# Softmax sums of two attention layers: from matmuls with ones to sums of exponentials along the query's row

## The chip, the cores and the metric

The kernel runs on one core of a Trainium2 chip. The metric is the device time in microseconds of one execution, as the median of several runs. A core has a matrix engine (TensorE, PE in the profile; PEld is its weight load), VectorE (DVE), ScalarE (ACT), GpSimd (POOL) and SyncE (SP), whose queue issues the DMAs here. Matrix results go to PSUM, of which there are eight banks of 128 partitions by 512 fp32 words; all else lives in SBUF.

## The reference

Four cross-attention layers follow each other on `x` (8 batches, 256 tokens, 512 features), with a context of the same shape. What matters here are the first layer and the fourth, which are ordinary attention with 16 heads of 32 features:

```python
# layer 0: layer norm, attention over the context, output projection, residual, then a feed-forward with gelu
scores = jnp.einsum('bhqd,bhkd->bhqk', q, k) * scale
scores = jnp.where(mask, scores, mask_value)
attn = jax.nn.softmax(scores, axis=-1)
out = jnp.einsum('bhqk,bhkd->bhqd', attn, v)
...
# layer 3: the context is layer-normed; Q from the hidden state, K and V from the context
scores = jnp.einsum('bhtd,bhsd->bhts', Q, K) * scale
scores = jnp.where(mask, scores, jnp.float32(-jnp.inf))
attn = jax.nn.softmax(scores, axis=-1)
out = jnp.einsum('bhts,bhsd->bhtd', attn, V)
return hidden_states + jnp.tanh(gate) * (out @ Wo.T)
```

The second layer is a single-head attention, the third has 32 query heads of 16 features on 8 key heads with an added mask.

## The kernel before

**Numbers in two parts.** Most products are done on pairs: a value is split into a rounded part and the rest (`hi`, `lo`), and three passes of matmuls join them (`feat_mm`, `tok_mm`).

**Units.** The attention of the first and fourth layer is cut into 32 units each, one for a batch and four heads (class `Mha`). `load` brings queries and keys of a unit into two tiles of the ring `stack` (in the fourth layer also `st` and `ks`), whose rows 0 to 95 hold the parts of the 32 features and whose further rows hold the mask and the maxima.

- `A(h)`, for each of the four heads: two matmuls give the scores of 256 queries (on partitions, in two halves) by 256 keys in an `sm` bank, of which there are two; VectorE takes the negative maximum of each query (`negm`, 128x2). After the last head GpSimd splits the eight columns of maxima into two parts (`mhl`).
- `B`: TensorE transposes `mhl`, ScalarE copies the result to `mT`, and a DMA writes it into rows 97 and 98 of the queries' tile, where the keys' tile holds ones.
- `C(i)`, four steps: matmuls give the scores again, now with keys on partitions and the maximum subtracted by the extra rows, in an `st` bank; ScalarE takes the exponential into the tile `P`. `P` of two heads and one half of the keys is one step.
- `AV(kt)`, one for each half of the keys: for each head the matmul of `P` with 32 columns of values into the bank `av`, columns 0 to 255, and a matmul of `P` with 32 columns of ones into columns 256 to 511: the sums of the softmax, repeated over the 32 partitions of the head. Each of these matmuls uses 32 columns of the array; four heads have four places side by side.
- `D`: the reciprocal of the sums (by Ln and Exp on ScalarE, or on VectorE while ScalarE's table for tanh is loaded), the product, and the split of the result into `at`, from which the projection of the batch is made.

The values stand in memory with their ones, 96 columns for two heads (`values`, `v0d`, `v3d`); the tile `V` holds 768 columns for each half of the keys.

**Order.** `pipeline` goes through the units: in step t it emits `A` of unit t, `B` of unit t-1 and `C` and `D` of unit t-2. `A` and `C` have a high priority; between them `fill.tick` emits filler work by a budget in microseconds (`B0` in the first layer, `B3` in the fourth): projections of later batches, the folded weights, the first feed-forward steps. The whole program is then put in order by a list scheduler with a model of the engines, so that the emitted order is a wish only. `Burst` asks it to issue the matmuls of a run one behind the other (`tc.issue_after` and a high priority). Each engine executes its own queue in order; an instruction that waits holds everything behind it on that engine.

**Slots.** SBUF is cut into named slots (a, b, c, v of fixed sizes); each phase has a table (`A0_SB`, `L_SB`, `L3_SB`) that says which slots a kind of tile goes through in turn. A tile's DMA or first write waits until the last reader of the slot's previous tile is done.

## Time and profile before

| | |
|---|---|
| median of 3 runs | 1755.96 us (1746.53, 1758.2, 1755.96) |
| profiled execution | 1749.14 us |
| its span, first to last instruction | 1747.4 us |
| mean granted clock of TensorE | 0.958 |
| TensorE / VectorE / ScalarE / GpSimd busy | 92% / 62% / 49% / 42% |
| value matmuls of the two layers (L588, 128x256) | 136.9 us busy, 2048 records |
| reductions to the maxima (L640) | 169.8 us, 256 |
| exponentials into `P` (L677) | 145.7 us, 256 |
| reciprocals on VectorE (L698) | 36.8 us, 21 |

How to read it: a busy time is the time in which at least one instruction of the group ran. Durations can overlap, on TensorE above all, so a mean duration times a count can be more than the busy time. "Idle before" is the time an engine stood still ahead of the group, with the instruction that released it. A row that begins with a time comes from the timeline: start and length in microseconds, engine, line, operation, tiles. Line numbers are those of the kernel before unless the text says that they belong to the changed one.

### The profile page before, as it was taken

The numbers are of one execution on the slowest core, as the hardware profiler recorded it, in microseconds if no ns is written. First come the engines' busy times: TensorE is split into PE (matmuls) and PEld (weight loads), VectorE is DVE, ScalarE is ACT, GpSimd is POOL, SyncE is SP. The second block draws the span as 40 slices with busy tenths as digits, with TensorE's granted clock in tenths as the row PEclk, the third lists the DMA queues.
The fourth block names the chain that finished last, engine by engine and source line by source line (L and its number), as shares of the span: only waits on it lengthen the run. The fifth ranks groups of instructions, "written<-read, shape, count | busy, mean of one in ns | idle before, by whom it ended". The sixth has DMA issues, their size and how long they took to land.

```text
span 1747.4 us, 28230 instructions
## 1 busy us (share of the span) xinstructions
PE 1616.0 (92%) x9984; PEld 1224.4 (70%) x9984; DVE 1085.8 (62%) x2412; ACT 864.0 (49%) x1531; POOL 731.1 (42%) x760
## 2 busy tenths in 40 slices
PE   7999999999799999999689899898878989999998
PEld 6877867777577878878456576666646767777765
DVE  6258557777757766622567577666777785655433
ACT  5336545554446566632255456454455545544444
POOL 6345145333455565531234445444436563422111
PEclk9999999999999999999789899898989999999999
DMA  8979775555632434285654575656366756776662
GB/s 294 319 240 285 220 234 190 164 153 164 188 129 88 146 119 145 77 290 218 196 175 151 190 240 174 202 177 189 97 198 180 231 164 217 213 220 210 192 182 76
DMA packets 168444, 329.16 MB, mean 188 GB/s; under 512 B 16336, under 2 KB 84336, under 8 KB 162800
## 3 DMA queue, kind: packets, MB, share of 16 engines
q1 hardware_dynamic: 168304, 327.35, 59.1%
q8 instruction: 80, 1.31, 0.3%
q14 instruction: 60, 0.49, 0.1%
HBM read 230.79 MB, written 96.49 MB: 187 GB/s over the span
## 4 chain that ended last, share of the span: by engine, by line
PE 64%; DMA 15%; DVE 9%; ACT 4%; issue 3%; POOL 3%; SPq 2%; DVEq 0%; ACTq 0%; POOLq 0%
PE pp L212 21%; PE pp L226 21%; PE av L588 8%; PE st L669 3%; PE sm L633 3%; PE st L1233 3%; PE sm L1179 2%; DMA stack<-mT 2%; DMA nat<-in_ctxT_dram 2%; DVE sm L1189 1%; DMA ws<-mnd 1%; PE pp L336 1%; PE pp L1143 1%; DMA stack<-q0d 1%; DMA nd<-avd 1%
## 5 line engine op out<-in xcount | busy, mean ns | idle before, releaser
L640 DVE TENSOR_REDUCE negm<-sm 128x2 f32<-128x512 f32 x256 | 169.8, 682 | 125.4 <-PE sm L633 124.7
L677 ACT ACTIVATE P<-st 128x512 f32<-128x512 f32 x256 | 145.7, 594 | 126.5 <-PE st L669 125.0
L212 PE MATMUL pp<-ys,fw 128*128 128x512 f32 x768 | 190.9, 398 | 6.3 <-ACT fw L178 3.8
L226 PE MATMUL pp<-pw,gs 128*128 128x512 f32 x768 | 193.3, 398 | 3.1 <-ACT gs L948 2.6
L212 PE MATMUL pp<-x,wq 128*128 128x256 f32 x1152 | 169.4, 291 | 6.9 <-ACT wq L181 3.1
L212 PEld LDWEIGHTS pp<-ys,fw 128*128 128x128 f32 x768 | 144.0, 191 | 40.4 <-ACT fw L178 4.0
L212 PEld LDWEIGHTS pp<-x,wq 128*128 128x128 f32 x1152 | 156.2, 196 | 20.5 <-issue 6.6
L226 PEld LDWEIGHTS pp<-pw,gs 128*128 128x128 f32 x768 | 142.1, 190 | 38.5 <-ACT gs L948 4.2
L588 PE MATMUL av<-P,V 128*32 128x256 f32 (+1 forms) x2188 | 164.5, 402 | 4.0 <-DVE xt L702 2.9
L1189 DVE CUSTOM_DVE_ANT_0 sm<-sm,va 128x256 f32<-128x256 f32 x256 | 104.8, 440 | 56.2 <-PE sm L1179 55.1
L1179 PE MATMUL sm<-ks,stack 96*128 96x512 f32 x256 | 111.4, 467 | 29.2 <-DMA stack<-q2d 16.3
L949 POOL TENSOR_TENSOR gs<-xt,gs 128x512 fp32r<-128x512 f32 x64 | 91.8, 1442 | 90.8 <-ACT gs L948 90.8
L1189 DVE CUSTOM_DVE_ANT_0 sm<-sm,vb 128x256 f32<-128x256 f32 x256 | 104.4, 440 | 37.8 <-PE sm L1179 36.5
L1233 PE MATMUL st<-stack,ks 100*128 100x512 f32 x256 | 103.7, 459 | 18.2 <-DMA stack<-mT 10.0
L1248 ACT ACTIVATE P<-P 128x1024 f32<-128x1024 f32 x90 | 95.1, 1059 | 50.3 <-POOL P L1244 26.0
L226 PE MATMUL pp<-wo,at 128*128 128x512 f32 x384 | 106.5, 404 | 1.3 <-ACT at L705 1.3
L944 DVE SCALAR_TENSOR_TENSOR xt<-xt,xt 128x512 f32<-128x512 f32 x64 | 66.6, 1045 | 64.5 <-ACT xt L943 64.5
L588 PEld LDWEIGHTS av<-P,V 128*32 128x32 f32 x2188 | 59.0, 109 | 57.6 <-issue 15.4
L179 POOL TENSOR_TENSOR fw<-stg,fw 128x1024 fp32r<-128x1024 f32 x32 | 81.8, 2564 | 34.7 <-ACT fw L178 19.6
L1179 PEld LDWEIGHTS sm<-ks,stack 96*128 96x128 f32 x256 | 51.5, 207 | 63.4 <-issue 30.0
L645 POOL CAST mhl<-negm 128x8 fp32r<-128x8 f32 x64 | 15.9, 249 | 187.7 <-DVE negm L640 187.7
L226 PEld LDWEIGHTS pp<-wo,at 128*128 128x128 f32 x384 | 69.8, 191 | 22.7 <-issue 3.3
(214 smaller groups left out, 3557.0 us busy)
## 6 DMA issues: line engine op xcount, KB each, us to landing
stg<-in_wfc_dram SPq DMA_DIRECT2D x32, 512.0 KB
stg<-in_wpr_dram SPq DMA_DIRECT2D x32, 512.0 KB
ws<-med SPq DMA_DIRECT2D x16, 1024.0 KB
ws<-mnd SPq DMA_DIRECT2D x16, 1024.0 KB
q2d<-nat SPq DMA_DIRECT2D x48, 256.0 KB
stack<-q2d SPq DMA_DIRECT2D x32, 384.0 KB
k0d<-nat SPq DMA_DIRECT2D x16, 512.0 KB
stack<-k0d SPq DMA_DIRECT2D x32, 256.0 KB
```

What stands on the lines that cost most here:

```text
L179: lo.tensor_tensor(w[:, 1], stg, fp(w[:, 0]), ALU.subtract)
L212: nc.tensor.matmul(pt[:, :n], lhsT=sel(ws, wj, kc)[:, ft * P : (ft + 1) * P], rhs=sel(xs, xj, kc), start=(k == 0), stop=(k == 11),)
L226: nc.tensor.matmul(pt[:, :n], lhsT=sel(xs, xj, kc)[:, tt * P : (tt + 1) * P], rhs=sel(ws, wj, kc), start=(k == 0), stop=(k == 11),)
L588: self.prev = nc.tensor.matmul(o, lhsT=lhsT, rhs=rhs, start=start, stop=stop, skip_group_check=True).ins
L640: nc.vector.tensor_reduce(self.negm[:, 2 * h : 2 * h + 2], pt.rearrange("p (q k) -> p q k", q=2), AX.X, ALU.max, negate=True)
L677: nc.scalar.activation(p, pt, AF.Exp)
L944: nc.vector.scalar_tensor_tensor(v, v, 1.0 / GA, u, ALU.add, ALU.mult)
L949: nc.gpsimd.tensor_tensor(lo, u, fp(hi), ALU.subtract)
L1179: nc.tensor.matmul(pts[qt], lhsT=self.qs[0:96, h, qt * P : (qt + 1) * P], rhs=self.ks[0:96].rearrange("p u k -> p (u k)"), start=True, sto ...
L1189: nc.vector.tensor_tensor_reduce(out=t, in0=t, in1=self.am[:, qt, :], scale=1.0, scalar=-3.0e38, op0=ALU.add, op1=ALU.max, accum_out=self. ...
L1233: nc.tensor.matmul(pt, lhsT=self.ks[0:100, u, kt * P : (kt + 1) * P], rhs=self.qs[0:100, 2 * hp : 2 * hp + 2, :].rearrange("p h t -> p (h ...
L1248: last["act"] = nc.scalar.activation(pf, pf, AF.Exp).ins
```

## The change

The sum of the exponentials is formed in `A`, where the scores stand with the queries on partitions: behind the reduction, ScalarE takes the exponential of each half of the bank with the negative maximum as its bias, back into the same bank, and writes the sum of the row (`sums`, 128x8 for a unit). `shift` takes the logarithm of the eight columns and subtracts it from the negative maximum; this difference is split into `mhl` and goes the way of the maximum's row. With it the exponentials in `C` give probabilities that add up to one, so the matmuls with ones, the reciprocal and the product are left out. While the table for tanh is loaded, the logarithm comes from an estimate by the bits of the number and a polynomial: nine VectorE operations on 128x8 and one exponential.

With it: `AV` goes into `D` as one run of eight matmuls, heads 0 to 3 for the first half of the keys, then for the second; the copy to `mT` and the first part of the result move from ScalarE to VectorE, the second part in the fourth layer from GpSimd to VectorE; the values lose their ones (512 columns instead of 768), in the fourth layer they come in two tiles in slots c0, c1, c3, c4, and `P` has five slots there instead of three; the mask's number is zero for a batch that is wholly masked.

```diff
@@ -55,7 +55,10 @@
     return o
 
 
-SMALL = dict(sm1=8, st6=4, negm=3, mhl3=3, mhl=2, mx=2, mT=3)
+SMALL = dict(sm1=8, st6=4, negm=3, sums=3, lg=6, mhl3=3, mhl=2, mx=2, mT=3)
+
+LN2 = 0.6931471805599453
+LGA, LGB = LN2 / 2.0**23, -LN2 * (127.0 - 0.0430357)
 C0_SB = dict(wk="a0-1", wv="a6-7", wq="a8-9", xs="a2-5", x8="a10-11", stg="b0-2", nat="b3-6", vo="b7-8,v0",
              h="b9-10", xt="c0-3", bc="c4-5", m="c6-8")
 A0_SB = dict(stack="a12-15", wc="a0-1", w8="a2-5", x8="a10-11", at="a6-7", stg="b3,b4,b6",
@@ -66,8 +69,8 @@
 L_SB = dict(wq="a12-13", wo="a0-1", ws="a8-9,a2", x8="a4-5,a3", ec="a6", pk="a7", at="a10-11", stack="a14-15",
             ks="b0,b1", P="b2,b6,b7", nat="b3,b4", h="b5,b10,b9,b8", nd="c0-1,c4", xt="c2", p1="c8",
             bc="c5-7", V="c3", va="v0", vb="v1")
-L3_SB = dict(L_SB, wk="a8-9", wv="a2,a7", x8="a4-5", st5="a3", vo="b3,b4", V="v0-1",
-             xt="c2", x32="c8")
+L3_SB = dict(L_SB, wk="a8-9", wv="a2,a7", x8="a4-5", st5="a3", vo="b3,b4", V="c0-1,c3-4",
+             P="b2,b6,b7,v0,v1", xt="c2", x32="c8")
 ALLP = list(range(8))
 PH_PS = dict(pp=[0, 1, 2], sm=[3, 4], st=[5, 6], av=[7])
 
@@ -427,9 +430,8 @@
     h1d = [dram([P, 2, D], "h1d") for _ in range(NB)]
     h2d = [dram([P, 2, D], "h2d") for _ in range(NB)]
     k0d, q0d, k3d, q3d = (nat_d(n) for n in ("k0d", "q0d", "k3d", "q3d"))
-
-    v0d = [dram([P, 2, 768], "v0d") for _ in range(NB)]
-    v3d = [dram([P, 2, 768], "v3d") for _ in range(NB)]
+    v0d = [dram([P, 2, D], "v0d") for _ in range(NB)]
+    v3d = [dram([P, 2, D], "v3d") for _ in range(NB)]
 
 
     q2d = [[dram([2, 96, 4, 256], "q2d") for _ in range(2)] for _ in range(NB)]
@@ -477,10 +479,13 @@
     nc.sync.dma_start(out=m8, in_=kmask)
     mrow = ph1.T([NB, 256], F, "m")
     nc.vector.tensor_copy(mrow, m8.bitcast(U8))
-    mb0 = ph1.T([NB, 256], R, "m")
-    nc.vector.tensor_scalar(mb0, mrow, 1.0, 2.0**100, ALU.subtract, ALU.mult)
     anyv = const.tile([NB, 1], F, name="anyv")
     nc.vector.tensor_reduce(anyv, mrow, AX.X, ALU.max)
+
+    big = const.tile([NB, 1], F, name="big")
+    nc.vector.tensor_scalar(big, anyv, 2.0**100, None, ALU.mult)
+    mb0 = ph1.T([NB, 256], R, "m")
+    nc.vector.tensor_scalar(mb0, mrow, 1.0, big, ALU.subtract, ALU.mult)
     anyv_d = dram([NB, 1], "anyv_d")
     nc.sync.dma_start(out=anyv_d, in_=anyv)
     anyb = const.tile([P, NB], F, name="anyb")
@@ -512,10 +517,9 @@
         for kt in range(2):
             pt = ph.PS("pp")
             c = tok_mm(pt, xs, tts + kt, wv)
-            V = ph.T([P, 8, 3, 32], F, "vo")
-            nc.gpsimd.memset(V[:, :, 1, :], 1.0)
-            nc.scalar.copy(V[:, :, 0:3:2, :], pt.rearrange("p (v x d) -> p v x d", x=2, d=32))
-            nc.sync.dma_start(out=vd[:, kt], in_=V.rearrange("p v x d -> p (v x d)"))
+            V = ph.T([P, D], F, "vo")
+            nc.scalar.copy(V, pt)
+            nc.sync.dma_start(out=vd[:, kt], in_=V)
             yield c
 
     TR = 8 * 2 * P * MMUS
@@ -627,7 +631,7 @@
         def A(self, h):
             ph, qs, ks = self.ph, self.qs, self.ks
             if h == 0:
-                self.negm = ph.T([P, 8], F, "negm")
+                self.negm, self.sums = ph.T([P, 8], F, "negm"), ph.T([P, 8], F, "sums")
             pt = ph.PS("sm")
             for qt in range(2):
                 nc.tensor.matmul(
@@ -640,10 +644,34 @@
             nc.vector.tensor_reduce(
                 self.negm[:, 2 * h : 2 * h + 2], pt.rearrange("p (q k) -> p q k", q=2), AX.X, ALU.max, negate=True
             )
+            for qt in range(2):
+                t, c = pt[:, qt * 256 : (qt + 1) * 256], slice(2 * h + qt, 2 * h + qt + 1)
+                nc.scalar.activation(t, t, AF.Exp, bias=self.negm[:, c], accum_out=self.sums[:, c])
             if h == 3:
-                m = self.mhl = ph.T([P, 2, 8], R, "mhl3")
-                nc.gpsimd.tensor_copy(m[:, 0], self.negm)
-                nc.gpsimd.tensor_tensor(m[:, 1], self.negm, fp(m[:, 0]), ALU.subtract)
+                self.shift()
+
+
+        def shift(self):
+            ph, negm, z = self.ph, self.negm, self.sums
+            y, nm = ph.T([P, 8], F, "lg"), ph.T([P, 8], F, "lg")
+            if self.ph is ph2 and tanh_table[0]:
+
+                d, t = ph.T([P, 8], F, "lg"), ph.T([P, 8], F, "lg")
+                nc.vector.tensor_scalar(y, z.bitcast(mybir.dt.int32), LGA, LGB, ALU.mult, ALU.add)
+                nc.scalar.activation(d, y, AF.Exp, scale=-1.0)
+                nc.vector.tensor_tensor(nm, negm, y, ALU.subtract)
+                nc.vector.tensor_tensor(d, d, z, ALU.mult)
+                nc.vector.tensor_scalar(d, d, 1.0, None, ALU.subtract)
+                nc.vector.tensor_scalar(t, d, -0.25, None, ALU.mult)
+                for c in (1.0 / 3.0, -0.5, 1.0):
+                    nc.vector.scalar_tensor_tensor(t, t, c, d, ALU.add, ALU.mult)
+                nc.vector.tensor_tensor(nm, nm, t, ALU.subtract)
+            else:
+                nc.scalar.activation(y, z, AF.Ln)
+                nc.vector.tensor_tensor(nm, negm, y, ALU.subtract)
+            m = self.mhl = ph.T([P, 2, 8], R, "mhl3")
+            nc.gpsimd.tensor_copy(m[:, 0], nm)
+            nc.gpsimd.tensor_tensor(m[:, 1], nm, fp(m[:, 0]), ALU.subtract)
 
 
         def B(self):
@@ -651,7 +679,7 @@
             mp = ph.PS("pp")
             nc.tensor.transpose(mp[0:16, 0:P], fp(self.mhl.rearrange("p j c -> p (j c)")), ident)
             mT = ph.T([32, P], R, "mT")[0:16]
-            nc.scalar.copy(mT, mp[0:16, 0:P])
+            nc.vector.tensor_copy(mT, mp[0:16, 0:P])
             nc.sync.dma_start(out=flat(self.qs)[97:99], in_=fp(mT))
 
 
@@ -675,38 +703,23 @@
                 )
             p = self.ps[kt][:, 2 * hp : 2 * hp + 2].rearrange("p h t -> p (h t)")
             nc.scalar.activation(p, pt, AF.Exp)
-            if i == 2:
-                self.AV(0)
-
-
-        def AV(self, kt):
+
+
+        def D(self):
             av, ft = self.av, self.ft
             with Burst() as mm:
-                for h in (2, 3, 0, 1):
-                    v = 192 * ft + 96 * (h // 2) + 64 * (h % 2)
-                    mm(av[32 * h : 32 * h + 32, 0:256], self.V[:, kt, v : v + 32], self.ps[kt][:, h], kt == 0, False)
-                for h in (2, 3, 0, 1):
-                    v = 192 * ft + 32
-                    mm(av[32 * h : 32 * h + 32, 256:512], self.V[:, kt, v : v + 32], self.ps[kt][:, h], False, kt == 1)
-
-        def D(self):
-            self.AV(1)
-            ph, av, ft = self.ph, self.av, self.ft
-            rc = ph.T([P, 2, 256], F, "xt")
-            r, o = rc[:, 0], rc[:, 1]
-            if self.ph is ph2 and tanh_table[0]:
-                nc.vector.reciprocal(r, av[:, 256:512])
-            else:
-                nc.scalar.activation(r, av[:, 256:512], AF.Ln)
-                nc.scalar.activation(r, r, AF.Exp, scale=-1.0)
-            nc.vector.tensor_tensor(o, av[:, 0:256], r, ALU.mult)
+                for kt in range(2):
+                    for h in range(4):
+                        v = 128 * ft + 32 * h
+                        mm(av[32 * h : 32 * h + 32, 0:256], self.V[kt][:, v : v + 32], self.ps[kt][:, h], kt == 0, kt == 1)
+            o = av[:, 0:256]
             hi, lo = self.at[ft // 2][:, 0, ft % 2, :], self.at[ft // 2][:, 1, ft % 2, :]
             if self.vbias is None:
-                nc.scalar.copy(hi, o)
-                nc.gpsimd.tensor_tensor(lo, o, fp(hi), ALU.subtract)
+                nc.vector.tensor_copy(hi, o)
+                nc.vector.tensor_tensor(lo, o, fp(hi), ALU.subtract)
             else:
                 bias = col(self.vbias, ft)
-                nc.scalar.activation(hi, o, AF.Identity, bias=bias)
+                nc.vector.tensor_scalar(hi, o, bias, None, ALU.add)
                 nc.vector.scalar_tensor_tensor(lo, o, bias, fp(hi), ALU.add, ALU.subtract)
 
         def E(self):
@@ -872,8 +885,9 @@
             wcs["w"] = load_w(ph2, wc0, "wc")
         if t % 4 == 0:
             fill.until(lambda: done0[0] >= b - 1)
-            V = ph2.T([P, 2, 768], F, "V")
+            V = ph2.T([P, 2, D], F, "V")
             nc.sync.dma_start(out=V, in_=v0d[b])
+            V = [V[:, 0], V[:, 1]]
             at = Lazy(ph2)
             for ft in range(4):
                 units0[t + ft].__dict__.update(V=V, at=at)
@@ -1465,8 +1479,9 @@
                 nc.gpsimd.memset(fp(t_[96:P]), 1.0)
         if ft == 0:
             fill.until(lambda: ready[0] > NB + b and k3n[0] > b)
-            V = ph6.T([P, 2, 768], F, "V")
-            nc.sync.dma_start(out=V, in_=v3d[b])
+            V = [ph6.T([P, D], F, "V") for _ in range(2)]
+            for kt in range(2):
+                nc.sync.dma_start(out=V[kt], in_=v3d[b][:, kt])
             at = Lazy(ph5)
             for i in range(4):
                 units[t + i].__dict__.update(V=V, at=at)
```

## The prediction

> **What bounds the kernel now.** I read the page first, then the busy time of the engines in four stretches, then the groups of instructions with shapes kept apart, then single places of the timeline. The page says that TensorE carries the kernel: it is busy 92% of the span, ScalarE half of it.
>
> ```profile
> span 1747.4 us, 28230 instructions
> ...
> PE 1616.0 (92%) x9984; PEld 1224.4 (70%) x9984; DVE 1085.8 (62%) x2412; ACT 864.0 (49%) x1531; POOL 731.1 (42%) x760
> ...
> PEclk9999999999999999999789899898989999999999
> ```
>
> A share over the whole span hides the stages. The first layer's attention (with projections and the first feed-forward steps as filler) runs from about 88 to 512 us, the third layer's about 850 to 1450, the fourth layer's from 1450. Columns: stretch, its length, busy time of PE, PEld, DVE, ACT, POOL, granted clock, DMA share, GB/s.
>
> ```profile
> 100.00:450.00 350.00, 334.42 (x2423) 258.66 (x2423) 240.00 (x367) 181.04 (x345) 143.33 (x151) 0.97 0.68 208
> 850.00:1450.00 600.00, 540.26 (x2939) 382.49 (x2943) 430.50 (x1437) 301.51 (x505) 279.21 (x286) 0.92 0.57 181
> 1450.00:1700.00 250.00, 246.21 (x2060) 189.07 (x2052) 128.79 (x219) 123.47 (x266) 67.04 (x125) 1.00 0.68 208
> 1700.00:1747.40 47.40, 39.34 (x361) 25.61 (x361) 16.64 (x29) 22.18 (x52) 6.94 (x17) 1.00 0.27 85
> ```
>
> In the two layers that change, TensorE is busy 95.5% and 98.5% at a clock of 0.97 and 1.00; ScalarE only 52% and 49%. The third layer, untouched, is the example of a stage whose other engines are fuller (DVE 72%): there TensorE has 90% and a clock of 0.92.
>
> **What is removed.** Per unit (one batch, four heads; 64 units in the two layers) 8 of 16 value matmuls go, those with the ones.
>
> ```profile
> L640 DVE TENSOR_REDUCE negm<-sm 128x2 f32<-128x512 f32 x256 | 169.8, 682 | 125.4 <-PE sm L633 124.7
> ...
> L588 PE MATMUL av<-P,V 128*32 128x256 f32 x2048 | 136.9, 385 | 2.9 <-DVE xt L702 2.9
> ...
> L698 DVE RECIPROCAL xt<-av 128x256 f32<-128x256 f32 x21 | 36.8, 1751 | 11.6 <-PE av L588 6.3 <-POOL ys L350 5.3
> ```
>
> 1024 matmuls appear as 2048 records and take 136.9 us. Half would be 68 us, 3.9% of the span: the tempting forecast. But these matmuls fill 32 of 128 columns and four run side by side, so their cost depends on how many stand together. The timeline (start, length) shows it:
>
> ```profile
> 1473.82 0.63 PE L588 MATMUL av<-P,V 128*32 128x256 f32 x4
> 1474.37 0.50 PE L633 MATMUL sm<-ks,stack 97*128 97x256 f32 x2
> 1474.80 1.06 PE L588 MATMUL av<-P,V 128*32 128x256 f32 x12
> 1475.79 0.39 PE L669 MATMUL st<-stack 99*128 99x256 f32 x1
> ```
>
> Two matmuls (4 records) hold TensorE for 0.55 us, six (12 records) for 0.99; the usual run of eight takes 1.00, of sixteen 1.86. Before, AV orders the heads 2, 3, 0, 1, so that a run begins with what is exponentiated last and then goes through. In the changed kernel D goes through heads 0 to 3 for each half of the keys, and the built instruction order lets a run begin as soon as its first two heads are ready. I counted runs in both orders: before 100 of eight, 11 of sixteen, 8 shorter; after 124 of two, 63 of four, 2 of six, for half as many matmuls. Before: 100 x 1.00 + 11 x 1.86 + 8 x about 0.8 = 127 us. After: 187 x 0.55 + 2 x 0.99 = 105 (four matmuls on four column groups cost as two on two). **Saving 22 us, not 68.** Bounds: the six 4-record runs last 0.33 to 1.00 us; at 0.33 the saving is 63. In the other direction 44 of the new runs contain a wait for ScalarE; half a microsecond each (one 128x512 exponential) would use the 22 up. I take 22, since 0.55 is where two of the six stand and the middle of them all.
>
> **What is added on ScalarE.** Eight exponentials of 128x256 with a sum per unit, 512 in all. The second layer has such instructions:
>
> ```profile
> 915.07 0.47 ACT L1113 ACTIVATE p<-pp,sm 128x256 f32<-128x256 f32 x1 [0.24 <-DVE sm L1109]
> 915.44 0.19 ACT L1113 ACTIVATION_READ_ACCUMULATOR p<-pp,sm 128x1 f32 x1
> 915.53 0.47 ACT L1113 ACTIVATE p<-pp,sm 128x256 f32<-128x256 f32 x1
> 915.89 0.20 ACT L1113 ACTIVATION_READ_ACCUMULATOR p<-pp,sm 128x1 f32 x1
> 915.98 1.05 ACT L1248 ACTIVATE P<-P 128x1024 f32<-128x1024 f32 x1
> ```
>
> Start to start it is 0.46 us, the sum's read included. In the new order 282 of the 512 wait for the instruction ahead on their own engine; 0.13 more each (0.59 until the read has ended). Per unit 8 x 0.46 + 4.4 x 0.13 = 4.25, and 0.2 for the logarithm of 128x8. Removed: the copy of the maxima's row 0.25 (L654), the copy of the result 0.51 (L709) or 0.41 (L705), and Ln and Exp 0.80 where they stood (43 of 64 units). First stretch, 30.5 units by its 122 reductions: 181 + 30.5 x 3.69 - 11 x 0.8 = 285 of 350 us. Fourth layer, 27.5 units: 123 + 27.5 x 2.99 = 206 of 250. ScalarE goes from half to 82% in both. Two more table loads (1.28 us each) stand in the new order. The new exponentials write back into PSUM in place, which no row of the trace does. The Trainium skill (ScalarE: Activation LUTs, "Step-by-step: what each stage is for") says that a PSUM destination is the quicker one for ScalarE; by it the 0.46 would be a ceiling, and the stages a little below 82%.
>
> **What is moved to VectorE.** First stretch: 21 reciprocals (37 us) and 30 products (0.415 each, 13) go; copies of the row (at most 0.29, the 128x128 eviction of L1062) add 9, the first half of the result (0.53, L348's 128x256 from PSUM) 16, and nine 128x8 operations in 18 units 28 to 87 us (0.174, the median of L1202, to 0.535, that of L1123). 240 becomes 243 to 302 of 350. Fourth layer: 129 becomes about 153 of 250. Idle time covers this; without it the row comes later, which is priced next. The memsets of ones (POOL, 0.31) and a third of the value bytes also go, off the path: nothing.
>
> **What the path gets instead.** (1) *The row comes later and is given less cover.* Reduction, row, transpose and DMA now have exponentials, the logarithm and up to nine small operations in front. Behind the transpose (L652) TensorE must have other work until the row has landed. Pricing TensorE's instructions between a unit's transpose and its first product of C (0.235 us for 512 columns, 0.118 for 256, 0.13 for a value matmul), the orders give, before and after: 7.3 and 5.7 us in the first layer, 7.7 and 4.5 in the fourth, 4.5 and 2.0 in its last eight units. The need is between 3.4 us (transpose 1709.49, product 1712.93, no wait reported) and 6.6 (0.9 for transpose and copy, and the DMA below, which was waited for):
>
> ```profile
> 1070.33 0.68 SPq L1213 DMA_DIRECT2D stack<-mT  x1
> ...
> 1076.03 0.47 PE L1233 MATMUL st<-stack,ks 100*128 100x512 f32 x1 [2.50 <-DMA stack<-mT]
> ```
>
> Summed shortfalls of all 64 units, after minus before: 25 us at a need of 3.4, 58 at 5.0, 90 at 6.6. The method overstates: at 5.0 it gives the kernel before 23 us, and its trace has one wait of 2.8 us. I take half of 58, **30 us**; bounds 0 and 90.
> (2) *The score banks are held longer.* There are two `sm` banks. Each was free after matmul and reduction (0.28 + 0.68); now two exponentials must pass ScalarE's queue as well, and the next A matmul stands ahead of all filler in TensorE's queue. The nearest row is the third layer, where TensorE waited 14 us for VectorE on these banks, over 256 tiles and at 72% load. Here are also 256 tiles, at 82%: **15 us**. Bounds: 0, and 40 if TensorE's share falls to the third layer's 90% in both stretches (350 x 0.055 + 250 x 0.085). If the clock falls to that layer's 0.92 too, 41 more (350 x (0.97/0.92 - 1) + 250 x (1/0.92 - 1)). The Trainium skill (TensorE: Matmul & The Clock Gate, "What's actually happening") ties the gate to idle windows of about 3.4 us; the waits above are shorter, so by the rule the clock would cost nothing. I leave it at nothing, and 41 in reach.
> (3) *A queue place.* The fourth layer's values now sit in slots c0 and c1 that the third layer's last results also use: in SP's order the last two `nd` loads stand 38 and 16 places later and wait for the new layer's value matmuls. Behind them are the last batch's projection and the slot that the fifth unit of the layer writes. **4 us**; 0 to 10.
> (4) *The end.* From the last value run (1738.33) to the product that needs it (1741.36) Ln, Exp, product and copy go and one copy stays: **-2**.
>
> **Sum.** 1749 (the profiled execution; its span is 1747.4) - 22 + 30 + 15 + 4 - 2 = 1774, that is 25 more. That execution was 7 us below the median 1756, so the forecast for a median is **1781 us**, chance 0.42.
>
> **The rivals.** *The products' saving comes through* (0.13): short runs cost 0.33 and the row is hidden by waits elsewhere. 1756 - 63 + 3 = 1696. For it: TensorE at 98.5% and DVE, POOL far from full. Against: 189 runs for 119. It decides if runs of two average under 0.4 us. *A wash* (0.29): saving 22, row 12, banks 8, the rest 2: 1756. For it: the overstated waits. *ScalarE sets the pace* (0.16): row 58, banks 40, clock part-way: 1756 - 22 + 98 + 8 = 1840. For it: 82% of a first-in-first-out queue that waits on two engines for each head; against: long stretches where filler needs little of ScalarE. It decides if ScalarE is over 90% busy in these layers.
>
> **How the numbers follow.** A measurement of this kernel can tell about 1% from no change, so 1738 to 1774 is the same. Range: the terms' spreads taken together (up 22, 60, 25 and 41, down 41, 30 and 15) rarely all fall on one side; 1722 to 1842 leaves 2 in 10 out. The faster rival gives 0.14, the wash 0.30, forecast and ScalarE's rival 0.56.
>
> **What would show it.** Value runs of 2 and 4 matmuls at 0.55 us and a sum near 105; ScalarE about 80% in both layers; TensorE's busy share in them down to about 90%, with waits for the `mT` load and for ScalarE on `sm` in its list. Wrong it is if value matmuls take under 75 us, or if TensorE stays above 95% in the fourth layer.

## The result, and the profile after

The changed kernel takes 1834.93 us (median of four runs, 1832.94 to 1836.50), the kernel before, in the runs beside it, 1751.24 us: a ratio of 1.0475, with a 95% interval of 1.0427 to 1.0523. That is 84 us slower, where 25 had been forecast. The profiled execution took 1835.2 us; its page:

```profile
span 1833.4 us, 27367 instructions
...
PE 1660.1 (91%) x8960; PEld 1227.8 (67%) x8960; DVE 1129.2 (62%) x2696; ACT 1056.6 (58%) x2407; POOL 693.5 (38%) x696
...
PEclk9989979999999999999789899999989987999978
```

TensorE has 1024 records fewer (512 matmuls) and is busy 44 us more. Its clock (0.934 in the mean, 0.958 before) now shows dips in both layers that change, which stood at 9 throughout. Three stretches, with the columns of before (length, PE, PEld, DVE, ACT, POOL, granted clock, DMA share, GB/s): the first layer, then the fourth in two parts.

```profile
100.00:480.00 380.00, 344.05 (x1968) 251.86 (x1966) 256.07 (x528) 273.28 (x755) 138.53 (x148) 0.93 0.60 187
1480.00:1700.00 220.00, 199.99 (x1290) 146.12 (x1289) 115.33 (x230) 151.48 (x462) 41.77 (x73) 0.95 0.58 176
1700.00:1825.00 125.00, 114.27 (x625) 71.97 (x623) 56.21 (x114) 85.68 (x274) 6.38 (x27) 0.88 0.36 107
```

TensorE has fallen to 91% in both layers. No other engine is full: ScalarE has 72% in the first layer and 69% in the fourth (237 of 345 us). The groups, shapes kept apart (busy, mean ns of one, idle time before and its releasers):

```profile
L649 ACT ACTIVATE sm<-sm,negm 128x256 f32<-128x256 f32 x512 | 231.6, 453 | 87.8 <-DVE negm L644 78.4 <-DVE sm L321 4.1 <-DVE lg L662 0.3
...
L644 DVE TENSOR_REDUCE negm<-sm 128x2 f32<-128x512 f32 x256 | 173.2, 686 | 155.7 <-PE sm L637 154.9
...
L592 PE MATMUL av<-P,V 128*32 128x256 f32 x1024 | 132.2, 412 | 2.8 <-ACT P L705 1.1 <-DVE at L719 0.7 <-DVE at L723 0.3
...
L637 PE MATMUL sm<-stack 97*128 97x256 f32 x320 | 69.0, 305 | 16.1 <-ACT sm L649 16.0
```

The row of L592: half the value matmuls are gone, and the rest keep TensorE busy for 132 us, against 137 before. The other three form a ring. ScalarE's new exponentials wait 78 us for maxima, VectorE's reductions 155 us for score matmuls (125 before), and the score matmuls for ScalarE. What TensorE, matmuls and weight loads together, waited for on the score banks, before (L633, for VectorE) and in the changed kernel (L637, for ScalarE), in us and times:

```profile
  DVE negm L640: 9.3, 16
...
  ACT sm L649: 55.1, 58
```

The timeline shows the ring turning, in the last units:

```profile
1774.19 0.80 PE L637 MATMUL sm<-ks,stack 97*128 97x256 f32 x2 [0.34 <-ACT sm L649]
...
1775.03 0.69 DVE L644 TENSOR_REDUCE negm<-sm 128x2 f32<-128x512 f32 x1 [0.24 <-PE sm L637]
...
1775.24 0.80 PE L637 MATMUL sm<-st 97*128 97x256 f32 x2 [0.26 <-ACT sm L649]
1775.75 0.45 ACT L649 ACTIVATE sm<-sm,negm 128x256 f32<-128x256 f32 x1 [0.56 <-DVE negm L644]
```

Read the brackets. TensorE waits for ScalarE to give a bank back, VectorE for TensorE's scores, TensorE for ScalarE again, ScalarE for VectorE's maximum: three engines, each in turn the one that is waited for. The pair of score matmuls takes 0.80 us here, where the granted clock was a half, and 0.40 at 1712.16, where it was full.

For the experiments the time is cut into three stages by the trace: to the last start of the feed-forward's second product (the first layer and its filler), from there to the last score matmul of the third layer (code that the change doesn't touch), and the rest (the fourth layer).

| kernel | median, us | ratio to before (95%) | first | middle | fourth |
|---|---|---|---|---|---|
| before | 1751 to 1758 | 1 | 799 | 635 | 313 |
| changed | 1834.9 | 1.0427 to 1.0523 | 834 | 639 | 361 |
| changed, whole value runs | 1832.7 | 1.0398 to 1.0466 | 829 | 643 | 356 |
| changed, early row | 1834.3 | 1.0410 to 1.0492 | 819 | 644 | 361 |
| changed, no exponentials for sums | 1737.9 | 0.9850 to 0.9931 | 792 | 626 | 312 |
| the same, whole value runs | 1721.9 | 0.9756 to 0.9855 | 792 | 630 | 297 |
| changed, half of the exponentials | 1753.4 | 0.9962 to 1.0004 | 789 | 631 | 328 |
| before, no products with ones | 1737.9 | 0.9844 to 0.9914 | 810 | 632 | 299 |

The loss stands where the change was made: 35 us in the first stage, 48 in the fourth. The middle stage, the same code in all, varies from 626 to 654 us over the experiments, because every edit gives the scheduler's order another shape; so differences of ten or fifteen microseconds in one stage of one kernel are not read here.

### The profile page after: what moved, and what is told of

Its sections match the earlier page's. It is cut to its first block, busy times and chain, and to the rows that moved or that the text cites. A ratio compares the mean times of both kernels' runs of the same rounds, so it can differ in the third digit from the quotient of the medians.

```text
span 1833.4 us, 27367 instructions
## 1 busy us (share of the span) xinstructions
PE 1660.1 (91%) x8960; PEld 1227.8 (67%) x8960; DVE 1129.2 (62%) x2696; ACT 1056.6 (58%) x2407; POOL 693.5 (38%) x696
## 5 line engine op out<-in xcount | busy, mean ns | idle before, releaser
L649 ACT ACTIVATE sm<-sm,negm 128x256 f32<-128x256 f32 x512 | 231.6, 453 | 87.8 <-DVE negm L644 78.4
L229 PE MATMUL pp<-pw,gs 128*128 128x512 f32 x768 | 199.2, 409 | 8.3 <-ACT gs L962 3.5
L229 PEld LDWEIGHTS pp<-pw,gs 128*128 128x128 f32 x768 | 147.5, 196 | 44.8 <-ACT gs L962 5.3
L592 PE MATMUL av<-P,V 128*32 128x256 f32 (+1 forms) x1164 | 159.6, 440 | 3.0 <-ACT P L705 1.1
L1193 PE MATMUL sm<-ks,stack 96*128 96x512 f32 x256 | 111.9, 471 | 30.9 <-DMA stack<-q2d 17.6
L673 POOL CAST mhl<-lg 128x8 fp32r<-128x8 f32 x64 | 13.2, 205 | 332.5 <-DVE lg L671 199.8
L1203 DVE CUSTOM_DVE_ANT_0 sm<-sm,vb 128x256 f32<-128x256 f32 x256 | 105.3, 439 | 43.2 <-PE sm L1193 41.8
L229 PE MATMUL pp<-wo,at 128*128 128x512 f32 x384 | 110.3, 415 | 1.6 <-DVE at L718 0.8
L1247 PE MATMUL st<-stack,ks 100*128 100x512 f32 x256 | 99.3, 448 | 11.8 <-DMA stack<-mT 5.4
L649 ACT ACTIVATION_READ_ACCUMULATOR sm<-sm,negm 128x1 f32 x512 | 105.3, 206 | 0.0
L182 POOL TENSOR_TENSOR fw<-stg,fw 128x1024 fp32r<-128x1024 f32 x32 | 81.6, 2562 | 34.4 <-ACT fw L181 34.4
```

What stands on the lines that cost most here:

```text
L182: lo.tensor_tensor(w[:, 1], stg, fp(w[:, 0]), ALU.subtract)
L229: nc.tensor.matmul(pt[:, :n], lhsT=sel(xs, xj, kc)[:, tt * P : (tt + 1) * P], rhs=sel(ws, wj, kc), start=(k == 0), stop=(k == 11),)
L592: self.prev = nc.tensor.matmul(o, lhsT=lhsT, rhs=rhs, start=start, stop=stop, skip_group_check=True).ins
L649: nc.scalar.activation(t, t, AF.Exp, bias=self.negm[:, c], accum_out=self.sums[:, c])
L1193: nc.tensor.matmul(pts[qt], lhsT=self.qs[0:96, h, qt * P : (qt + 1) * P], rhs=self.ks[0:96].rearrange("p u k -> p (u k)"), start=True, sto ...
L1203: nc.vector.tensor_tensor_reduce(out=t, in0=t, in1=self.am[:, qt, :], scale=1.0, scalar=-3.0e38, op0=ALU.add, op1=ALU.max, accum_out=self. ...
```

## Experiments: the value matmuls

**Whole runs.** `D` begins with what is exponentiated last, so that nothing in a run has to be waited for:

```diff
-                for kt in range(2):
-                    for h in range(4):
+                for kt in (1, 0):
+                    for h in (2, 3, 0, 1):
                         v = 128 * ft + 32 * h
-                        mm(av[32 * h : 32 * h + 32, 0:256], self.V[kt][:, v : v + 32], self.ps[kt][:, h], kt == 0, kt == 1)
+                        mm(av[32 * h : 32 * h + 32, 0:256], self.V[kt][:, v : v + 32], self.ps[kt][:, h], kt == 1, kt == 0)
```

> The changed kernel, but a unit's eight value matmuls begin with what is exponentiated last (second half of the keys, heads 2, 3, 0, 1; then the first half), so that in the built order 63 of 65 runs hold all eight. Theory (the saved products brought nothing because their runs were broken into pieces of two and four, 132 us busy for half as many matmuls): the value matmuls fall to 64 to 72 us, and as TensorE carries the layers most of it reaches the end: 1835 - 40 to 65 = 1770 to 1795 us. Rival (waits for ScalarE and for the row set the pace, TensorE only fills the time between): busy time falls as well, but the time stays within 10 us of 1835.

```profile
L592 PE MATMUL av<-P,V 128*32 128x256 f32 x1024 | 77.6, 418 | 13.0 <-ACT P L705 13.0
...
L637 PE MATMUL sm<-stack 97*128 97x256 f32 x320 | 70.8, 313 | 14.9 <-ACT sm L649 11.5 <-DMA stg<-in_wfc_dram 3.1
```

This group row is of that kernel: 55 us of TensorE's time are gone, and the time is 1832.7 us, 2 us less than the changed kernel's, which is nothing. TensorE's share falls from 91% to 88%, and its waits for ScalarE on the score banks grow from 55 to 77 us. The rival was right: with the new exponentials in place, it is not TensorE's time that sets how long these layers last.

**Before, without the products with ones.** The ones' eight matmuls of a unit are left out, and the normaliser comes from the other half of the bank, by one operation for each that was there (an Exp stands in for the Ln).

```diff
-                for h in (2, 3, 0, 1):
-                    v = 192 * ft + 32
-                    mm(av[32 * h : 32 * h + 32, 256:512], self.V[:, kt, v : v + 32], self.ps[kt][:, h], False, kt == 1)
...
-                nc.vector.reciprocal(r, av[:, 256:512])
+                nc.vector.reciprocal(r, av[:, 0:256])
```

> The kernel before without its products with ones (the normaliser is taken from the other half of the bank by operations of the same sizes). Value matmuls in its own order: 94 runs of four, 17 of eight. Theory (runs of four cost 0.55 us, and TensorE carries the layers): value matmuls 69 to 80 us, time 1756 - 45 to 65 = 1690 to 1710 us. Rival (TensorE's time is waited away elsewhere): above 1735.

1737.9 us, ratio 0.988: a gain of some 20 us for 55 us of TensorE (136.9 to 81.6). That is the rival's time (above 1735), though a part of the saving does arrive. In the profiled executions the clock falls from 0.958 to 0.940, and TensorE's whole busy time by 25 us only (1616 to 1591): some 30 of the 55 us come back as other matmuls that take longer. Even alone, the tempting half of this change was worth 1.2%, not 3.9%.

**Whole runs, once ScalarE is relieved.** The edit of the whole runs, on the kernel without the sums' exponentials (the sums a constant; next section):

> The kernel without the sums' exponentials (sums a constant 2.0), its eight value matmuls in one run that begins with what is exponentiated last. If TensorE carries these layers once ScalarE is relieved, the shorter time of whole runs (77 us busy against 106) now reaches the end: 1738 - 15 to 30 = 1708 to 1723 us. If short runs only fill time that TensorE would wait anyway: 1733 to 1745 us.

1721.9 against 1737.9 us: 16 us (12 between the profiled executions, whose fourth stage falls from 312 to 297). So run order does pay where the exponentials are out of the way. The value matmuls were 106.0 us busy there in broken runs and 74.6 in whole ones.

**Whole runs in the kernel before.** All sixteen value products of a unit, those with ones too, in one run behind the last exponential; no other edit:

```diff
-            if i == 2:
-                self.AV(0)
...
+        def D(self):
+            av, ft = self.av, self.ft
+            with Burst() as mm:
+                for kt in (1, 0):
+                    for h in (2, 3, 0, 1):
+                        v = 192 * ft + 96 * (h // 2) + 64 * (h % 2)
+                        mm(av[32 * h : 32 * h + 32, 0:256], self.V[:, kt, v : v + 32], self.ps[kt][:, h], kt == 1, False)
+                    for h in (2, 3, 0, 1):
+                        v = 192 * ft + 32
+                        mm(av[32 * h : 32 * h + 32, 256:512], self.V[:, kt, v : v + 32], self.ps[kt][:, h], False, kt == 0)
```

> The kernel before with all sixteen value products of a unit (those with ones too) in one run that begins with what is exponentiated last; no other edit, sums by products as before. Whole runs gave 16 us where TensorE carries the layers. If that holds here (64 runs of sixteen at 1.86 us are 119 us, against 127 to 137 us): 1735 to 1750 us. If the later start of the first half of the products costs as much: 1753 to 1765 us.

1738.8 us, ratio 0.990 (0.984 to 0.996): a whole kernel that is faster than both, by the order of its matmuls alone. Its value matmuls are busy 125.4 us, 11.5 less than before, and the time falls by 18 us against the runs beside it, by 10 between the profiled executions.

## Experiments: the row, the exponentials and the banks

**Without the exponentials.** The 512 exponentials with sums are left out, the sums are a constant 2.0; logarithm, subtraction and row stay:

```diff
-            for qt in range(2):
-                t, c = pt[:, qt * 256 : (qt + 1) * 256], slice(2 * h + qt, 2 * h + qt + 1)
-                nc.scalar.activation(t, t, AF.Exp, bias=self.negm[:, c], accum_out=self.sums[:, c])
+            if h == 0:
+                nc.gpsimd.memset(self.sums, 2.0)
```

> The changed kernel without the 512 exponentials of the sums; the sums are a constant 2.0, the logarithm and the rest stay. Takes away ScalarE's 0.46 us each, the hold of the score banks and that part of the row's delay. Theory (ScalarE's queue between score matmul and row costs the largest share of the 84 us, part of it through the clock): 1750 to 1785 us, clock back to 0.95 or more, waits on the sm banks nearly gone. Rival (the short value runs and the small operations of the logarithm are the loss): 1810 to 1835.

1737.9 us: below the range of both theories. These 512 instructions cost 97 us, and everything else in the change together is a gain of 13 to 20 (against 1751 and 1758).

**An early row.** `shift` takes the maxima alone, so the row waits for no sum and no logarithm; the exponentials stay, their sums unused:

```diff
-            y, nm = ph.T([P, 8], F, "lg"), ph.T([P, 8], F, "lg")
...
+            ph, nm = self.ph, self.negm
             m = self.mhl = ph.T([P, 2, 8], R, "mhl3")
```

> The changed kernel with all its exponentials and sums, but the row is made of the maxima alone, so it waits neither for the sums nor for a logarithm, whose operations are left out. ScalarE's load and the hold of the banks stay. If the lateness of the row is the main loss: 1775 to 1800 us. If the banks and ScalarE's load are: 1815 to 1835, with the waits of score matmuls on ScalarE as before it (some 55 us).

1834.3 us, the changed kernel's time. With the exponentials in place the lateness of the row costs nothing that can be measured here (the intervals are some 8 us wide to either side).

**Half of the exponentials** (one of a head's two query tiles; the other sums are 2.0):

```diff
-            for qt in range(2):
+            if h == 0:
+                nc.gpsimd.memset(self.sums, 2.0)
+            t, c = pt[:, 0:256], slice(2 * h, 2 * h + 1)
+            nc.scalar.activation(t, t, AF.Exp, bias=self.negm[:, c], accum_out=self.sums[:, c])
```

> The changed kernel with half of the sums' exponentials: one of the two query tiles of each head, the other sums a constant 2.0. If each exponential costs its share of the path: halfway, 1775 to 1800 us. If ScalarE costs nothing until its queue is nearly full: 1738 to 1765 us.

1753.4 us. The first 256 cost 15 us, the second 256 cost 82. That is no price by the piece; it looks like a limit that is reached, as the second theory had it. Whether of the banks or of ScalarE's queue this run can't tell, since it takes from both.

**The bank's hold without ScalarE's time, and the other way round.** First, one ScalarE operation of 128x2 on the bank in place of a head's two exponentials:

```diff
+            nc.scalar.activation(scr, pt[:, 0:512:256], AF.Identity, bias=self.negm[:, 2 * h : 2 * h + 1])
```

> The changed kernel with one ScalarE operation of 128x2 per head on the score bank in place of two exponentials of 128x256 with sums (the sums are a constant 2.0): the bank is still given back only by ScalarE behind the maximum, but ScalarE's load for it falls from some 270 us to some 55. If ScalarE's time costs: 1735 to 1765 us. If the round trip over ScalarE's queue before a bank is free costs, whatever its length: 1800 to 1835 us.

1764.4 us, 26 more than without the exponentials and within the first theory's range. Much of it is in the middle stage: the stages of the profiled execution are 799, 654 and 316, so in the two layers it costs 11 us (799 + 316 against 792 + 312). Giving the bank back by a short way over ScalarE costs little. Second, the kernel of the early row with operations that read a constant in SBUF and write to SBUF, behind their maximum as before, so that only the bank is free (and with two `mT` tiles instead of three, as in the next two kernels):

```diff
-                nc.scalar.activation(t, t, AF.Exp, bias=self.negm[:, c], accum_out=self.sums[:, c])
+                nc.scalar.activation(
+                    scr[qt].rearrange("p (q k) -> p q k", q=2), ident.unsqueeze(1).to_broadcast([P, 2, P]),
+                    AF.Identity, bias=self.negm[:, c], accum_out=self.sums[:, c],
+                )
```

> The kernel with the early row (maxima alone), its 512 ScalarE operations with sums kept, each still behind its maximum, but reading a constant in SBUF (Identity in place of Exp) and so holding no score bank. If the held banks are what costs the 97 us between the kernel without the sums' exponentials and the changed one: 1740 to 1765 us. If ScalarE's own time and queue are: 1815 to 1840 us.

1792.8 us, between the two theories: 55 over the kernel without exponentials, 42 under that of the early row. Its stages are 824, 638 and 334. The last value run of the first layer starts at 508 us here, at 507 without exponentials, at 534 with the early row and at 540 in the changed kernel: with the bank free the first layer's attention is on time. Its stage is not: 824 us, against 819 with the bank held and 792 without exponentials. The bank's part shows in the fourth stage, 334 against 361 (312 without exponentials); in the first stage ScalarE's operations cost as much without the bank. One thing was not tried apart: these operations also leave PSUM alone, where the exponentials read and write it.

**Is it the wait or the time?** Two kernels were to take ScalarE's wait for the maximum away from the last one.

```diff
-                    AF.Identity, bias=self.negm[:, c], accum_out=self.sums[:, c],
+                    AF.Identity, accum_out=self.sums[:, c],
```

> The kernel with the early row and 512 ScalarE operations on a constant, now without the wait for the maximum (no bias): ScalarE's time alone, neither bank nor wait for VectorE. With the wait it took 1793 us. If ScalarE's queue standing still behind a reduction is the cost: 1740 to 1765 us. If its time alone is: 1780 to 1800 us.

1766.2 us, but it missed its aim: with nothing to wait for, the scheduler put all 512 operations ahead of 423 us, none in the fourth layer. What it shows is that double the number of them costs the first stage 30 us (822 against 792) when they hold nothing and wait for nothing. With the wait, half as many cost it 32.

```diff
-            for qt in range(2):
-                c = slice(2 * h + qt, 2 * h + qt + 1)
+            for i in ((), (0, 1), (0, 1), (0, 1, 0, 1))[h]:
+                c = slice(2 * h - 2 + i, 2 * h - 1 + i)
```

> The kernel with the early row and 512 ScalarE operations on a constant that hold no bank (1793 us), but each behind the maximum of the head before, which is there already when its turn comes. The run without any bias was to show the same and missed it: all its operations ran before 423 us. If ScalarE standing behind a reduction was the cost: 1745 to 1770 us. If its time is: 1785 to 1800 us.

1803.4 us. This one kept them spread, but ScalarE waited 32.9 us for maxima, against 28.6 in the kernel it was to relieve. Neither tells wait from time.

**Three score banks.** First with a third bank in the two layers that the projections use too (`sm=[3, 4, 2]`), then, in all layers, with one of its own, which leaves the projections two, and that with and without the exponentials:

```diff
-PH_PS = dict(pp=[0, 1, 2], sm=[3, 4], st=[5, 6], av=[7])
+PH_PS = dict(pp=[0, 1], sm=[2, 3, 4], st=[5, 6], av=[7])
```

> The changed kernel with three banks for the scores (the third is shared with the projections). If two score banks are too few for the longer hold: 1770 to 1800 us, waits of score matmuls on ScalarE from some 55 us down to under 20. If ScalarE's time sets the pace: 1825 to 1840 us; above that the projections miss the bank.

1926.2 us, although TensorE's waits for ScalarE on the score banks fall from 55 to 30 us. The likely reason is that the projections miss the bank they share, which was not shown apart; on its question the run says nothing.

> The changed kernel with three score banks of its own and two for projections instead of two and three (in all layers). Read against the next kernel, which has the same banks without the sums' exponentials; with two score banks the difference of the pair was 97 us. If the held banks make the round trip costly: a difference of 35 to 65 us. If it is ScalarE's time or its waits: 85 to 105 us.

> The kernel without the sums' exponentials (sums a constant 2.0), with three score banks and two for projections: the base for the kernel with the same banks and all exponentials. Two projection banks cost the filler something: 1738 to 1800 us by both theories.

1880.4 and 1828.8 us. With a projection bank gone both are slow (without exponentials 91 us slower than with three projection banks), but their difference is 52 us where it was 97. About half of the cost goes when a bank of their own is added. The step of the constant in SBUF gave 42 for the same thing by another way; and here too more of it is in the fourth stage, whose difference falls from 48 to 29 us, than in the first, from 42 to 33. Two reservations: the pair's base is slower, and a slower kernel hides more; and with three banks the score matmuls still wait 43 us for ScalarE, so the ring is not gone.

**Relief for ScalarE.** In both layers the evictions and casts of the filler were moved to VectorE and GpSimd:

```diff
-            nc.scalar.copy(w[:, 0], stg)
+            (nc.gpsimd.tensor_copy if relief[0] else nc.scalar.copy)(w[:, 0], stg)
...
-                    nc.scalar.copy(hi, u)
+                    hcopy(hi, u)
...
+    def hcopy(o, i):
+        if relief[0]:
+            nc.vector.tensor_copy(o, i)
+        else:
+            nc.scalar.copy(o, i)
```

> The changed kernel, with ScalarE relieved of other work while the two layers run: casts of weights go to GpSimd, evictions and casts of projections, values and the feed-forward's first half to VectorE. ScalarE's busy time in 100 to 480 us falls from 273 to about 200, in the fourth layer by some 25 of 237. If the sum of ScalarE's work is the cost (half of the exponentials cost only 15 us), the first layer's 32 us shrink to under 15 and the time is 1795 to 1818 us. If the exponentials cost by their own chain (maximum, two exponentials, next score matmul), whatever else ScalarE does: 1828 to 1845 us.

```profile
100.00:480.00 380.00, 328.39 (x1815) 244.78 (x1815) 261.69 (x548) 196.66 (x597) 156.03 (x168) 0.89 0.56 172
```

1863.7 us, slower than either theory. The line is its first layer: ScalarE is down from 273 to 197 of 380 us. ScalarE's waits in that stretch (total, times, longest):

```profile
ACT sm L649 <- DVE negm L644: 30.9, 30, 3.2
...
ACT sm L660 <- DVE negm L655: 104.7, 54, 6.8
```

The first line is the changed kernel, the second this one: 104.7 us for maxima, where there were 30.9. Most of that is not a later maximum. By the starts and ends in the two traces a reduction begins 0.89 us in the mean behind its score matmuls (0.77 in the changed kernel), and its first exponential 0.33 us behind it (0.64): ScalarE, with less else to do, is there sooner and waits. A score bank is held 3.6 us in the mean of this stretch, from its first matmul to the end of its last reader, against 4.1 in the changed kernel and 2.3 before. So in this stage banks that are given back sooner did not bring time either, and TensorE's waits for ScalarE on them grow, over the whole kernel, from 55 to 93 us; why, the runs don't tell. Then the casts of weights alone, to GpSimd:

> The changed kernel with the casts of weights alone (128x1024, about 33 us of ScalarE in 100 to 480 us) on GpSimd while the two layers run; VectorE keeps its work. In the run that relieved ScalarE of all evictions ScalarE waited 105 us for maxima in VectorE's queue, and the first stage (to the end of the feed-forward) grew from 834 to 862 us. If the first layer's loss is ScalarE's time: that stage shrinks to 805 to 825 us and the time to 1805 to 1825 us. If it is the round trip over the maximum: stage within 6 us of 834, time 1828 to 1842 us.

1848.0 us, the first stage 843: no gain from ScalarE's time here either (235 of 380 us busy, waits for maxima 48.0). So less work for ScalarE by itself brought nothing. That it is not the limit is not shown, since in both kernels the work moved to engines that the units need too: GpSimd, with the casts, also splits the row. Why these kernels became slower, and not the same, the runs don't tell.

**The clock.** 48 more matmuls, read by nothing, in the last three batches' `C`:

```diff
+            if self.ph is not ph2 and self.b >= NB - 3:
+                nc.tensor.matmul(
+                    ph.PS("pp"), lhsT=qs[0:97, 2 * hp, 0:P], rhs=ks[0:97, 2 * hp : 2 * hp + 2, :].rearrange("p h t -> p (h t)"),
+                    start=True, stop=True,
+                )
```

> The changed kernel with one matmul of 512 columns on data at hand added in each step C of the fourth layer's last three batches (48 in all, some 20 us of TensorE's time), whose result nothing reads. If the lower clock of these units (0.88 from 1700 to 1825 us) is itself the cost and comes from TensorE's gaps: clock over 0.93 there and 1815 to 1830 us. If the clock only follows the waits: 1835 to 1855 us.

```profile
1700.00:1825.00 125.00, 117.08 (x675) 75.49 (x674) 55.83 (x114) 85.27 (x271) 6.41 (x27) 0.96 0.35 104
```

The same stretch as in the changed kernel: the clock is back from 0.88 to 0.96, TensorE has done some 20 us more work over these units (48 at 0.4 us), and the time is 1835.1 us, unchanged. The gaps and the faster matmuls together took that work in, and nothing was left over as time. What the clock alone would give, without the added work, this can't tell; that 55 us less of TensorE's work bought nothing (whole runs) speaks against much.

## Why the prediction was wrong

The direction and the range (1722 to 1842) held; the amount did not: 84 us measured, 25 forecast. Term by term:

- **Value matmuls, -22.** Wrong in the changed kernel: 136.9 to 132.2 us busy, and even 55 us less of them bought nothing (whole runs). The runs came as they were counted (124 of two, 63 of four, 2 of six), and a run of two costs what one of four does: 0.63 and 0.64 us in the trace (median, to the end of its last matmul), where one of eight before took 1.07. By these times 189 runs are 121 us; 22 of them fell into stretches at half the clock and took 1.03 in the mean, and all came to 132. The 105 of the forecast was counted from start to start, as the 127 beside it was. The 106 us of the kernel without exponentials are near it by luck: there the runs were 148, with fewer short ones. But the step from TensorE's time to the kernel's time assumed that TensorE still sets the end. Together with the rest of what was taken out and moved it is worth 13 to 20 us, as the kernel without exponentials shows.
- **The later row, +30.** Nothing: the early row changed the time by 0.6 us. The method, which added up cover behind the transposes, was said to overstate, and it did so wholly, at least beside a larger loss.
- **The score banks held longer, +15, bounds 0 and 40.** This is the step that failed. The price came from the third layer, where TensorE waits 14 us for VectorE on as many banks: the same count of tiles, but another ring. By the same view TensorE waited 55 us here, and in time the exponentials cost 97 us. Some 42 to 45 of that hang on the held bank (constant in SBUF; three banks, 97 - 52), most of it in the fourth layer. The other 52 to 55 remain when ScalarE's operations hold no bank, or when the scores have a third, and for these the sum had no term: it had ScalarE at 82% and priced the banks alone. Whether they cost by their time or by their wait for the maximum could not be told apart, and why work taken off ScalarE brought nothing stays open.
- **The clock, left at nothing with 41 in reach.** It fell to 0.93 and 0.95, and 0.88 at the end. The Trainium skill (TensorE: Matmul & The Clock Gate, "What's actually happening") ties the gate to idle windows of about 3.4 us, and by it, as it was read, the clock should have stayed. The trace shows both: at 1542 us the clock falls behind a wait of 4.6 us, but at 1767 us no single wait of the 8 us ahead was over 0.9 us, and it was granted by half for the next 20 us. These are TensorE's last three waits ahead of that fall, and the stretches on both sides of it, whose clock reads 1.00 and then 0.50:

```profile
1764.59 0.50 PE L637 MATMUL sm<-stack,ks 97*128 97x256 f32 x2 [0.88 <-ACT sm L649]
1765.64 0.50 PE L637 MATMUL sm<-stack,ks 97*128 97x256 f32 x2 [0.55 <-ACT sm L649]
1766.67 0.79 PE L697 MATMUL st<-stack 99*128 99x256 f32 x4 [0.53 <-DMA stack<-mT]
...
1759.00:1767.00 8.00, 5.77 (x36) 3.42 (x37) 5.55 (x12) 6.48 (x24) 0.39 (x2) 1.00 0.66 203
1767.20:1787.60 20.40, 19.51 (x73) 10.94 (x72) 7.93 (x17) 13.90 (x47) 0.78 (x4) 0.50 0.28 80
```

So the measurement disagrees with that reading of the rule. The forecast of no cost is nevertheless not shown to have failed: where the clock was restored, with more matmuls, the time stayed.
- **The queue place, +4, and the end, -2.** Too small to be told: no run takes them apart, and order alone moves a stage by more.

What was forecast for TensorE came out, about 90% in both layers. ScalarE stayed below its 82%, at 72 and 69%, and VectorE, 256 of 380 us, below its 243 to 302 of 350: the layers took longer, so the same work is a smaller share. Such shares do not show a ring.

Of the rivals, the one that came nearest in time was that ScalarE sets the pace (1840 us, chance 0.16). Its own condition, ScalarE over 90% busy, was not met. That its time was near is therefore luck in part. Three engines at 67 to 91% (the first layer) can still set the pace when each waits for the next, with two banks to keep them apart. A threshold fits this better than a sum: half of the exponentials 15 us, all of them 97.

## What to carry to other kernels

When a new step is put between a matmul's result and the release of its PSUM bank, price the whole way round (matmul, each reader, the queues ahead of each reader) against the number of banks, and not by the busy share alone of the engine that gets the work; and look for a threshold, with half of the step as a trial. Work taken off a matrix engine at 95% is worth what it frees only as long as that engine still sets the end: here 55 us of it were worth 20 in one kernel, 16 of 31 in another and 2 of 55 in the third. Column-tiled matmuls that run side by side should be issued in one run, last-ready operand first; that alone gave the kernel before 1% (0.4 to 1.6), and the changed one nothing.

## What the runs showed of the hardware

- A ScalarE exponential of 128x256 within PSUM took 448 ns (median), and the same size as Identity with the same kind of bias from SBUF to bf16 in SBUF 499 ns, without the bias 410 ns. Reading the sum adds 0.2 us each: 105.3 us for 512 of them.
- The granted clock fell to a half at 1767 us of the changed kernel though no wait in the 8 us ahead was over 0.9 us, and 48 matmuls of 512 columns that nothing reads were enough to bring the last stretch from 0.88 to 0.96.
- A cast of 128x1024 took 1.04 us on GpSimd in most cases (some up to 1.50, in the kernel with the casts there) and 1.05 on ScalarE.
